# Cross-attention and a mixture of experts on one core: partial sums kept in PSUM by ScalarE copies, and another order of products, silu parts and expert sums

## Chip, core and metric

One core of one Trainium2 chip. The metric is device microseconds of that core for one launch of the kernel. The core's engines are TensorE (PE; its weight loads are PEld), VectorE (DVE), ScalarE (ACT), GpSimd (POOL) and SyncE (SP), which issues the loads and stores. Each runs its own list of instructions in order and waits for the others by semaphores. Matmul results land in PSUM, which has eight banks; all else that engines read lies in SBUF.

## What is computed

x has 16 rows of 112 tokens with 256 features, `ctx` 16 rows of 375. First cross-attention, then a mixture of 8 experts in which every expert is applied to every token:

```
q = layernorm(x) @ Wq + bq;  k = ctx @ Wk + bk;  v = ctx @ Wv + bv
x = x + softmax(q k^T / 16) v
z = layernorm(x)
cw = softmax(z w_router) * softmax(z w_gating / 0.1);  cw = cw / (sum(cw) + 1e-9)
h_e = silu(z w_gate[e]) * (z w_up[e])          # 256 -> 1024, for e = 0..7
x = x + sum_e cw[:, e] * (h_e w_down[e])       # 1024 -> 256
```

## The kernel before

**The head.** `Line` is a small planner: every operation of the attention, of routing and of the first products is declared with an engine, a cost, a priority and what it reads and writes, and `Line.run` writes out an order for each engine from these. `batch(b)` declares the attention of one row: scores, the largest score (`top`, L931), the shift (`low`, L934), the exponential (L938), the transposed probabilities (L944), the mixed context (L957), projection and residual (L972, L979), layer norm and its transposed copy. `port=True` tells the planner that VectorE and GpSimd can't do this beside each other. `top`, `low`, `cs` and `total` are small SBUF tiles.

**The expert steps.** The 1792 tokens are two halves (h) of 896. A step is (expert e, half h, block j of 256 hidden features, m): m = 0 is the gate, m = 1 the up projection; 8 x 2 x 4 x 2 = 128 steps. In a step the product of a 896 x 256 and a 256 x 256 matrix is done with seven products of half-size blocks instead of eight (a scheme of Strassen's kind): `PROD` says which block or sum of blocks of x (`X_...`) and of the weights (`W_...`) go into each. Each product is three matmuls of 448 columns, because every operand is split into a high and a low part (`hi`, `lo`) and the products high-high, low-high and high-low are summed (`PASSES`). The four blocks of the result are

```
(0,0) = P1 + P2            (0,1) = P1 + P6 + P5 + P3   # c12
(1,1) = P1 + P6 + P7 + P5  (1,0) = P1 + P6 + P7 + P4   # c22, c21
```

Before, `step` issues the products in the order 1, 6, 5, 2, 7, 4, 3. ScalarE copies P1 to SBUF (`v1`, L542); VectorE adds up `w16` = P1 + P6 (L547), `u3` = w16 + P7 (L568), `c22` = u3 + C (L570, bank C holds P5), `c21` (L582) and, when P3 has been added in bank C, `c12` (L592). Block (0,0) is summed in bank A by the matmuls. In a gate step ScalarE applies silu to each block (L469); in an up step VectorE multiplies the silu parts by the up blocks (L559, L584, L494), ScalarE casts the result to its high part `hhi` (L488, L495) and VectorE subtracts for the low part `hlo` (L489, L496). What is not done at once is kept in `carry` and issued later by `finish`.

**Down products.** After each up step 14 groups (7 token tiles t, 2 feature halves F) are queued in `downs`; a group is three matmuls of 256 columns (L402). `fill(k)` puts k groups between the products of later steps, seven a step; `KEEP` groups stay in the queue. They sum over the four j in four banks D0 to D3, two token tiles a bank. When an expert's half is complete, `gather` adds it with its weight `cw` to `acc`, on VectorE (L421) or, with `aside`, by ScalarE (L418) and GpSimd (L419).

**Weights.** `plan` sets when a weight is loaded (`raw`), its block sums are formed on GpSimd (`t`, L320 to L323), its high part is cast on ScalarE (`hi`, L335) and its low part subtracted on GpSimd (`lo`, L341); the same for `w_down` (L348, L350). In the first expert one weight is prepared in each step; weights 0 to 2 (`EARLY`) are prepared in the head. `REST` and `offer` slip pieces of the second half's x sums and splits into the first steps.

Of the kernel before, what the change touches and what calls it, by code (L numbers as in the profile page):

```python
# [143 lines left out]
def kernel(  # L144
# [65 lines left out]
    AHEAD = {"w": 16, "d": 16, "hhi": 48, "hlo": 32}  # L210
# [148 lines left out]
    for k in range(NW):  # L359
        e, i = divmod(k, PER)  # L360
        if e == 0:
            if i < EARLY:
                continue
            n = i - 2
            plan(n - 1, "raw", k)
        else:
            n = 2 * PER * (e - 1) + PER + (2, 4, 6, 7, 8, 10, 12, 13)[i]
            plan(n - 2, "raw", k)
        plan(n if e == 0 else n - 1, "t", k)
        plan(n, "hi", k)  # L370
        plan(n + 1, "lo", k)
# [37 lines left out]
    def gather(bank, aside=False):  # L409

        if len(done.get(bank, ())) < min(2, NTT - 2 * bank):
            return
        for h, e, t, pd in done.pop(bank):
            tt = h * NTT + t
            w = cw[:, tt, e : e + 1]
            if aside:
                y = buf("y", [P, D], f"y{h}_{e}_{t}")
                nc.scalar.activation(y, pd, AF.Copy, scale=w)  # L418
                nc.gpsimd.tensor_add(acc[tt], acc[tt], y)  # L419
            else:  # L420
                nc.vector.scalar_tensor_tensor(  # L421
                    acc[tt], pd, w, acc[tt], op0=ALU.mult, op1=ALU.add
                )
        if e == E - 1:
            t0 = (h * NTT + 2 * bank) * P
            a = accs[h, bank]
            nc.sync.dma_start(
                out_f[t0 : t0 + a.shape[1] * P, :].rearrange("(t p) d -> p t d", p=P), a
            )
# [11 lines left out]
    KEEP = 6  # L441
# [25 lines left out]
    def silu(n, blk, src):  # L467
        s = tmp("s", f"{n}s") if blk == (0, 0) else src
# [22 lines left out]
    def put_off(hid, blk, src):  # L491
        s = sg[blk]
        hi, lo = parts(hid, blk)
        carry["hf%d%d" % blk] = lambda: nc.vector.tensor_mul(s, s, src)  # L494
        carry["hhi%d%d" % blk] = lambda: nc.scalar.copy(hi, s)  # L495
        carry["hlo%d%d" % blk] = lambda: nc.vector.tensor_sub(lo, s, f(hi))  # L496

# [11 lines left out]
    def step(n):  # L509
        e, h, j, m = steps[n]  # L510
        up = m == 1
        for what in ("lo", "raw", "rawd", "t"):
            due(n, what)
        hi_now = list(todo.get((n, "hi"), ()))
        todo.pop((n, "hi"), None)
# [5 lines left out]
        if up:  # L521
            hid = [
                (
                    buf("hhi", [P, HT], f"hhi{n}_{F}", FR),
                    buf("hlo", [P, HT], f"hlo{n}_{F}", FR),
                )
                for F in range(2)
            ]
        pb, pc, pe = (psum(t, f"p{t}{n}")[:, :N] for t in "BCE")
        if n > 1:  # L530
            pa = psum("A", f"pA{n}")[:, :N]
        finish("hf10", "hf01")
        if up:
            finish("hlo11")
            gather(1)
        offer()
        if n == 1:
            pa, v1 = e0["pa1"], e0["v11"]
        else:
            prod(n, pa, 1, True, False)  # L540
            v1 = tmp("v1", n)
            nc.scalar.copy(v1, pa)  # L542
        finish("silu01", "hhi10", "hhi01")
        offer()
        prod(n, pb, 6, True, True)
        w16 = tmp("s", f"{n}w")
        nc.vector.tensor_add(w16, v1, pb)  # L547
        if up:
            finish("hlo10")
            newest[0] = n  # L550
        else:
            finish("hlo00", "hlo01")
            gather(2, True)
        hi(0)
        prod(n, pc, 5, True, False)
        fill(1, not up)
        prod(n, pa, 2, False, True)
        if up:
            nc.vector.tensor_mul(sg[(0, 0)], sg[(0, 0)], pa)  # L559
            hi(1)  # L560
            due(n, "d")
        else:
            silu(n, (0, 0), pa)
            gather(3, True)
            hi(1)
# [4 lines left out]
        nc.vector.tensor_add(c22, u3, pc)  # L570
        offer()
        fill(2)
        offer()
        fill(1)
        if up:
            keep_hidden(hid, (0, 0))
        else:
            gather(0)
            silu(n, (1, 1), c22)
        prod(n, pb, 4, True, True)  # L580
        c21 = u3
        nc.vector.tensor_add(c21, u3, pb)  # L582
        if up:
            nc.vector.tensor_mul(sg[(1, 1)], sg[(1, 1)], c22)  # L584
            keep_hidden(hid, (1, 1))
        else:
            silu(n, (1, 0), c21)
        offer()
        fill(2)
        prod(n, pc, 3, False, True)  # L590
        c12 = w16
        nc.vector.tensor_add(c12, w16, pc)  # L592
        fill(1)
        offer()
        if up:
            for blk, src in (((1, 0), c21), ((0, 1), c12)):
                put_off(hid, blk, src)
        else:
            carry["silu01"] = lambda: silu(n, (0, 1), c12)
        if up:  # L600
            T_OF = (range(0, 3), range(4, NTT), range(3, 4))
            order = [(0, t) for t in T_OF[0]]
            order += [(1, t) for t in T_OF[1]]
            order += [(0, t) for t in T_OF[1]] + [(0, 3)]
            order += [(1, t) for t in T_OF[0]] + [(1, 3)]
            if n == len(steps) - 1:
                order.append(order.pop(order.index((0, NTT - 1))))
            seen = set()
            for F, t in order:
                last = j == NJ - 1 and t in seen  # L610
                seen.add(t)

                downs.append((n, h, e * NJ + j, 1 - F, t, hid[F], j == 0, last))
# [34 lines left out]
    top, low, total = (many(n, B) for n in ("top", "low", "total"))  # L648
# [248 lines left out]
    def batch(b):  # L897
# [10 lines left out]

        def turn(k):
# [11 lines left out]
        def score():  # L921
            for k in range(KC):
# [8 lines left out]
           lambda: nc.vector.reduce_max(top[:TQ, col], bank(("sc", b), [TQ, TK]), axis=AX.X, negate=True),  # L931
# [3 lines left out]
               low[:TQ, col], top[:TQ, col], cs[:TQ, col], cs[:TQ, col], op0=ALU.subtract, op1=ALU.add),  # L935
           reads=(("mx", b), ("c", g)), writes=(("nb", b),), port=True)
# [199 lines left out]
    for k in range(EARLY):  # L1136
# [7 lines left out]
        for part in range(2):  # L1144
            op("POOL", (1.02, 1.31)[part], pri, lambda k=k, part=part: load_lo(k, part),
               reads=(("wh", k), ("raw", k), ("t", k)), writes=(("w", k),))
    op("SP", 0.45, 9, lambda: load_rawd(0), writes=("rawd",), waits=("bq", "bk"), kb=256)
# [42 lines left out]
    def silu0():  # L1190
        silu(0, (0, 0), e0["A"])
# [20 lines left out]
    op("PE", 0.61, 31, second, reads=(("w", 1), ("xs", 0, X_A11)), new=(("bank", ("second",), BANKS[4:]),))  # L1212
    op("ACT", 0.54, 31, v1_second, reads=(("second",), "v1"), writes=("v11",), waits=[("aT", B - 1), ("aTl", B - 1)])
# [7 lines left out]
    def later(what, *blocks):  # L1221
# [3 lines left out]
        1: [later(sum_x, X_S1), later(split_hi, X_A22), later(split_hi, X_S1), later(sum_x, X_S2),  # L1225
            later(split_lo, X_A22, X_S1), later(split_hi, X_S2)],
        2: [later(sum_x, X_S3), later(split_lo, X_S2), later(split_hi, X_S3), later(sum_x, X_S4),
            later(split_hi, X_S4)],
        4: [later(split_lo, X_S3), later(split_lo, X_S4)],
# [8 lines left out]
    for n in range(1, len(steps)):  # L1238
        if n in REST:
            waiting.append(parts_of(REST[n]))  # L1240
        step(n)
# [3 lines left out]
    finish("hlo00", "hf10", "hlo11", "hhi10", "hf01", "hhi01", "hlo10", "hlo01")  # L1245
# [41 lines left out]
```

## Time and profile before

| | |
|---|---|
| runs (median; lowest to highest) | 989.07 us; 988.94 to 991.05 |
| profiled execution: time / span | 990.8 us / 989.0 us |
| busy: TensorE / VectorE / ScalarE / GpSimd | 972.8 / 804.3 / 504.7 / 415.7 us |
| matmuls | 6059 |
| granted TensorE clock, mean | 0.998 |

The profile is one execution. A row of the groups names line, engine, operation, output and inputs by the program's names, the shape, the count, busy time and the mean length. The chain that ended last is followed back from the last instruction to whatever released each. A row of the waits is: who waited, for whom, total us, times, longest. A row of a timeline is: start us, length us, engine, line, operation. Successive matmuls overlap: a 448-column matmul is listed with 0.36 us while the next starts 0.20 us later.

### The profile page before, as it was taken

Reading aid. Unit: us, or ns where it says so; the run is one execution under the profiler, and the core shown is the slowest. Engines: PE = TensorE matmul, PEld = TensorE weight load, DVE = VectorE, ACT = ScalarE, POOL = GpSimd, SP = SyncE. Lnnn points to the kernel's source line nnn. Section 1 sums busy time; section 2 is a strip of 40 time slices with the busy share of each in tenths; the row PEclk is TensorE's granted clock in tenths of the full one; section 3 lists DMA queues with packets and bytes.
Section 4 is the critical chain, followed back from the end, with each engine's and each line's share of the span. In section 5 each row is a group of like instructions: output and inputs, shape, how many; then the busy total and the mean of one; then the engine's idle time right before and its main releaser. Section 6 shows DMA issues by size and latency. Waiting matters only on the chain.

```text
span 989.0 us, 16353 instructions
## 1 busy us (share of the span) xinstructions
PE 972.8 (98%) x6059; PEld 907.4 (92%) x6059; DVE 804.3 (81%) x1506; ACT 504.7 (51%) x1037; POOL 415.7 (42%) x524
## 2 busy tenths in 40 slices
PE   9999879999999999999999999999999999999998
PEld 6887769999999999999999999999999999999997
DVE  5778798878888888888887887878888888788786
ACT  5676654455444554555445544456455545455342
POOL 3346483255414561446324550555244632455000
PEclk9999999999999999999999999999999999999999
DMA  9611111001100110011100110011001110010011
GB/s 238 178 48 36 31 43 44 12 22 54 43 2 22 54 33 22 22 33 43 32 12 22 54 44 1 23 54 32 22 22 33 43 32 12 22 44 1 1 38 38
DMA packets 36053, 38.66 MB, mean 39 GB/s; under 512 B 3251, under 2 KB 33974, under 8 KB 35974
## 3 DMA queue, kind: packets, MB, share of 16 engines
q1 hardware_dynamic: 35696, 37.37, 13.1%
q8 instruction: 47, 0.77, 0.3%
q14 instruction: 32, 0.26, 0.1%
q10 hardware_dynamic: 278, 0.27, 0.1%
HBM read 33.95 MB, written 1.84 MB: 36 GB/s over the span
## 4 chain that ended last, share of the span: by engine, by line
PE 94%; DVE 3%; ACT 1%; issue 1%; DMA 0%; POOL 0%; DVEq 0%
PE pd L402 32%; PE pC L436 16%; PE pB L436 15%; PE pA L436 15%; PE pE L436 8%; PE ps_aa L957 2%; PE ps_sc L923 2%; PE ps_qk L869 1%; PE ps_po L972 1%; PE ps_cT L911 1%; PE ps_pp L944 0%; DVE low L934 0%; DMA wn<-in_L_xattn_Wq_dram 0%; PE ps_lg L1048 0%; PE ps_xT L856 0%
## 5 line engine op out<-in xcount | busy, mean ns | idle before, releaser
L402 PE MATMUL pd<-wd,hhi 128*128 128x256 f32 x1792 | 338.8, 280 | 0.0
L402 PEld LDWEIGHTS pd<-wd,hhi 128*128 128x128 f32 x1792 | 308.9, 188 | 14.2
L402 PE MATMUL pd<-wd,hlo 128*128 128x256 f32 x896 | 250.8, 280 | 1.7 <-DVE hlo L489 1.7
L436 PE MATMUL pC<-xs_hi,w 128*128 128x448 f32 x508 | 187.8, 370 | 3.5 <-DVE s_1c L570 0.8
L436 PE MATMUL pB<-xs_hi,w 128*128 128x448 f32 x508 | 186.7, 368 | 0.0
L436 PE MATMUL pA<-xs_hi,w 128*128 128x448 f32 x504 | 183.0, 363 | 0.0
L402 PEld LDWEIGHTS pd<-wd,hlo 128*128 128x128 f32 x896 | 169.2, 189 | 2.0 <-DVE hlo L489 1.9
L419 POOL TENSOR_TENSOR acc<-acc,y 128x256 f32<-128x256 f32 x45 | 35.8, 824 | 247.6 <-ACT y L418 247.6
L341 POOL TENSOR_TENSOR w<-raw,w 128x384 fp32r<-128x384 f32 x64 | 72.8, 1138 | 135.9 <-ACT w L335 135.9
L542 ACT COPY v<-pA 128x448 f32<-128x448 f32 x126 | 67.0, 532 | 89.2 <-PE pA L436 89.2
L436 PEld LDWEIGHTS pC<-xs_hi,w 128*128 128x128 f32 x508 | 95.6, 188 | 14.5 <-DVE s_1c L570 1.2
L436 PEld LDWEIGHTS pB<-xs_hi,w 128*128 128x128 f32 x508 | 96.0, 189 | 5.8 <-DVE s_1u L582 0.2
L436 PEld LDWEIGHTS pA<-xs_hi,w 128*128 128x128 f32 x504 | 94.5, 187 | 4.0 <-ACT v L542 0.3
L436 PE MATMUL pC<-xs_lo,w 128*128 128x448 f32 x254 | 92.7, 365 | 0.0
L436 PE MATMUL pE<-xs_hi,w 128*128 128x448 f32 x254 | 92.5, 364 | 0.0
L436 PE MATMUL pB<-xs_lo,w 128*128 128x448 f32 x254 | 92.1, 363 | 0.0
L436 PE MATMUL pA<-xs_lo,w 128*128 128x448 f32 x252 | 90.9, 361 | 0.0
L341 POOL TENSOR_TENSOR w<-tt,w 128x512 fp32r<-128x512 f32 x64 | 83.1, 1298 | 2.1
L350 POOL TENSOR_TENSOR wd<-rawd,wd 128x512 fp32r<-128x512 f32 x32 | 41.7, 1304 | 72.2 <-ACT wd L348 72.2
L436 PEld LDWEIGHTS pE<-xs_hi,w 128*128 128x128 f32 x254 | 47.7, 188 | 3.2
L436 PEld LDWEIGHTS pC<-xs_lo,w 128*128 128x128 f32 x254 | 47.9, 189 | 1.5
L436 PEld LDWEIGHTS pB<-xs_lo,w 128*128 128x128 f32 x254 | 47.7, 188 | 1.6
(1812 smaller groups left out, 1898.9 us busy)
## 6 DMA issues: line engine op xcount, KB each, us to landing
raw<-in_L_ffn_w_gate_dram SPq DMA_DIRECT2D x32, 256.0 KB
raw<-in_L_ffn_w_up_dram SPq DMA_DIRECT2D x32, 256.0 KB
rawd<-in_L_ffn_w_down_dram SPq DMA_DIRECT2D x32, 256.0 KB
ctx<-in_ctx_dram SPq DMA_DIRECT2D x13, 336.0 KB
out_dram<-acc SPq DMA_DIRECT2D x6, 256.0 KB
wide<-in_x_dram SPq DMA_DIRECT2D x3, 448.0 KB
wide<-in_ctx_dram SPq DMA_DIRECT2D x3, 336.0 KB
ctx<-in_ctx_dram SPq DMA_DIRECT2D x13, 39.0 KB
```

Source lines behind the costliest of these rows:

```text
L341: nc.gpsimd.tensor_sub(wts[k][1][:, d], w, f(wts[k][0][:, d]))
L350: nc.gpsimd.tensor_sub(wds[q][1], rawds[q], f(wds[q][0]))
L402: nc.tensor.matmul(pd, hs[a][:, t * P : (t + 1) * P], wds[q][w][:, fi, :], start=(opening and s == 0), stop=(last and s == 2), skip_group_ ...
L419: nc.gpsimd.tensor_add(acc[tt], acc[tt], y)
L436: nc.tensor.matmul(ps, w_[w][:, wi, :], (xs_hi, xs_lo)[a][h][xi], start=(start and s == 0), stop=(stop and s == 2), skip_group_check=True,)
L542: nc.scalar.copy(v1, pa)
L869: nc.tensor.matmul(bank(("qk", g, m, 0), [P, GT]), m_sb[:, k, m * P : (m + 1) * P], xnT_b[k], start=(k == 0), stop=(k == KC - 1),)
L911: nc.tensor.transpose(bank(("cT", b, k), [P, TK])[:, c * KT : (c + 1) * KT], ct()[:, c, k * P : (k + 1) * P], ident[:KT, :KT],)
L923: nc.tensor.matmul(bank(("sc", b), [TQ, TK]), own(qk_b[k], ("qk", g, k))[:, i * TQ : (i + 1) * TQ], ctT(k), start=(k == 0), stop=(k == KC ...
L957: nc.tensor.matmul(bank(("aa", b), [P, KC, TQ])[:, k, :], ct()[:, c, k * P : (k + 1) * P], pT()[:, c, :], start=(c == 0), stop=(c == NK - 1),)
L972: nc.tensor.matmul(bank(("po", b), [TQ, D]), aT()[:, a, k, :], (wv_hi, wv_lo)[w][:, k, :], start=(k == 0 and s == 0), stop=(k == KC - 1 an ...
```

## The change

- In a step from the third on, ScalarE copies bank A (P1) into bank B, and P6 is added there by its matmuls; ScalarE copies bank B (P1 + P6) into bank E, where P7 and, after `c22` has been read, P4 are added. VectorE no longer adds `u3` and `c21`; it copies bank B to SBUF (`w16`), ScalarE copies P5 to SBUF (`p5`), and VectorE forms `c12` = w16 + C and `c22` = p5 + E. Block (1,0) is read from bank E.
- The order of products is 1, 5, 6, 2, 3, 7, 4; the down groups stand as two after 5, one after 3, four after 7. In a gate step only groups of older pairs are used.
- The second step (n = 1) has its own function, `second_step`, with sums in SBUF as before.
- The low parts of the hidden blocks are subtracted in other places, most of them in the next gate step; `put_off` is gone.
- `gather` is always VectorE's; the calls stand elsewhere. The order of the 14 down groups is another one; `KEEP` is 7.
- In the head `top` lies in the scores' own bank instead of SBUF, `low` reads it there, and `low` is declared without `port`. Weight 3 is loaded and its block sums are formed in the head; in the first expert `raw` and `t` come a step earlier. `REST` starts at step 3.

In the built order of the new program TensorE has as many matmuls as before; VectorE's list has 204 instructions fewer, ScalarE's 204 more, GpSimd's 45 fewer. VectorE's copy `w16` waits for ScalarE's copy of bank B to bank E. In the head GpSimd's sums of weight 3 stand between the low part of weight 1 and the next row statistics.

```diff
-    AHEAD = {"w": 16, "d": 16, "hhi": 48, "hlo": 32}
+    AHEAD = {"w": 32, "d": 16, "hhi": 48, "hlo": 32}
...
             n = i - 2
-            plan(n - 1, "raw", k)
+            if i > EARLY:
+                plan(n - 2, "raw", k)
...
-        plan(n if e == 0 else n - 1, "t", k)
+        if k > EARLY:
+            plan(n - 1, "t", k)
...
-    KEEP = 6
+    KEEP = 7
...
+    def leave(hid, blk):
+        hi, lo = parts(hid, blk)
+        s = sg[blk]
+        carry["hhi%d%d" % blk] = lambda: nc.scalar.copy(hi, s)
+        carry["hlo%d%d" % blk] = lambda: nc.vector.tensor_sub(lo, s, f(hi))
+
+    def hide(blk, src):
+        nc.vector.tensor_mul(sg[blk], sg[blk], src)
...
     def step(n):
         e, h, j, m = steps[n]
         up = m == 1
+        hi, hid = begin(n)
+        pb, pc, pe = (psum(t, f"p{t}{n}")[:, :N] for t in "BCE")
+        pa = psum("A", f"pA{n}")[:, :N]
+        if up:
+            gather(2)
+            gather(3)
+        offer()
+        prod(n, pa, 1, True, False)
+        nc.scalar.copy(pb, pa)
+        offer()
+        prod(n, pc, 5, True, False)
+        p5 = tmp("v1", f"{n}p5")
+        nc.scalar.copy(p5, pc)
+        if up:
+            newest[0] = n
+        else:
+            if n > 2:
+                finish("hhi11", "hlo00", "hlo01")
+            gather(0)
+        fill(2, not up)
+        prod(n, pb, 6, False, True)
+        nc.scalar.copy(pe, pb)
+        w16 = tmp("v1", f"{n}w")
+        nc.vector.tensor_copy(w16, pb)
+        if n == 2:
+            hi(0)
+        finish("hhi01", "hhi11", "hhi10")
+        if n > 2:
+            hi(0)
+        offer()
+        prod(n, pa, 2, False, True)
+        if up:
+            hide((0, 0), pa)
+            hi(1)
+            due(n, "d")
+        else:
+            silu(n, (0, 0), pa, False)
+            hi(1)
+        prod(n, pc, 3, False, True)
+        c12 = tmp("s", f"{n}c12")
+        nc.vector.tensor_add(c12, w16, pc)
+        offer()
+        fill(1, not up)
+        prod(n, pe, 7, False, False)
+        if up:
+            keep_hidden(hid, (0, 0))
+        else:
+            silu(n, (0, 1), c12)
+        c22 = tmp("s", f"{n}c22")
+        nc.vector.tensor_add(c22, p5, pe)
+        offer()
+        if up:
+            hide((0, 1), c12)
+            keep_hidden(hid, (0, 1))
+        else:
+            finish("hlo00", "hlo01", "hlo11", "hlo10")
+        fill(4, not up)
+        if not up:
+            gather(1)
+        prod(n, pe, 4, False, True)
+        if up:
+            hide((1, 1), c22)
+            leave(hid, (1, 1))
+            hide((1, 0), pe)
+            leave(hid, (1, 0))
+            queue_downs(n, hid)
+        else:
+            silu(n, (1, 1), c22)
+            silu(n, (1, 0), pe, False)
+        offer()
...
+        order = [(0, t) for t in range(3)] + [(1, t) for t in range(NTT)] + [(0, t) for t in range(3, NTT)]
...
+        top = lambda: bank(("sc", b), [TQ, 512])[:, TK : TK + 1]
...
-               low[:TQ, col], top[:TQ, col], cs[:TQ, col], cs[:TQ, col], op0=ALU.subtract, op1=ALU.add),
-           reads=(("mx", b), ("c", g)), writes=(("nb", b),), port=True)
+               low[:TQ, col], top(), cs[:TQ, col], cs[:TQ, col], op0=ALU.subtract, op1=ALU.add),
+           reads=(("sc", b), ("mx", b), ("c", g)), writes=(("nb", b),))
...
+    op("SP", 0.45, 11, lambda: load_raw(EARLY), new=(("raw", ("raw", EARLY)),), kb=256)
+    op("POOL", 1.9, 29.5, lambda: load_t(EARLY), reads=(("raw", EARLY),), new=(("tt", ("t", EARLY)),))
...
-        1: [later(sum_x, X_S1), later(split_hi, X_A22), later(split_hi, X_S1), later(sum_x, X_S2),
-            later(split_lo, X_A22, X_S1), later(split_hi, X_S2)],
-        2: [later(sum_x, X_S3), later(split_lo, X_S2), later(split_hi, X_S3), later(sum_x, X_S4),
-            later(split_hi, X_S4)],
-        4: [later(split_lo, X_S3), later(split_lo, X_S4)],
+        3: [later(sum_x, X_S1, X_S2), later(split_hi, X_A22, X_S1), later(split_lo, X_A22), later(sum_x, X_S3),
+            later(split_hi, X_S2), later(sum_x, X_S4)],
+        4: [later(split_lo, X_S1), later(split_hi, X_S3), later(split_lo, X_S2), later(split_hi, X_S4),
+            later(split_lo, X_S3), later(split_lo, X_S4)],
...
-        step(n)
+        step(n) if n > 1 else second_step()
```

## Prediction

> **What bounds the kernel now.** I read the page first. TensorE is busy for 98% of the span and is 94% of the chain that ended last, so the change can win only where TensorE stands still, and it can lose wherever a new wait opens.
>
> ```profile
> PE 972.8 (98%) x6059; PEld 907.4 (92%) x6059; DVE 804.3 (81%) x1506; ACT 504.7 (51%) x1037; POOL 415.7 (42%) x524
> ...
> PE 94%; DVE 3%; ACT 1%; issue 1%; DMA 0%; POOL 0%; DVEq 0%
> ```
>
> Next the chain in order of time (start, length, what). A run of nine down matmuls occurs once per step, so the distance between two of them is a step.
>
> ```profile
> 206.91 1.06 PE pd L402 x9
> 213.62 1.06 PE pd L402 x9
> 220.33 1.06 PE pd L402 x9
> 227.24 1.06 PE pd L402 x9
> 233.95 1.06 PE pd L402 x9
> ```
>
> A step takes 6.71 us, and now and then 6.9. Successive matmuls of a product start 0.20 us apart and down matmuls 0.118 us (1.06/9), so a step's bare work is 21 x 0.20 + 21 x 0.118 = 6.68 us: it has no room. From 153 us to the end 15 steps are long, by 0.175 us on average: 2.6 us. In each of the two per expert, the multiply of L584 took 1.61 us instead of 0.62 while GpSimd ran, the add of L592 behind it came late, and the next product 5 waited for bank C.
>
> Then TensorE's waits (total, times, longest). They lie almost all between 93 and 149 us, where attention ends and the expert steps begin.
>
> ```profile
> PE ps_sc L923 <- DVE s L628: 2.3, 2, 1.4
> PE pd L402 <- DVE hlo L489: 1.7, 1, 1.7
> ...
> PE ps_pp L944 <- ACT s L938: 0.9, 1, 0.9
> PE pC L436 <- DVE s_1c L570: 0.8, 1, 0.8
> PE ps_first_C L436 <- DVE s_0c L1177: 0.8, 1, 0.8
> PE pC L436 <- DVE s_3c L570: 0.8, 1, 0.8
> PE pC L436 <- DVE s_3w L592: 0.7, 1, 0.7
> ```
>
> Last the timeline of VectorE around 100 us, then GpSimd's in the same stretch.
>
> ```profile
> 100.24 3.66 DVE L934 SCALAR_TENSOR_TENSOR low<-top,cs 112x1 f32<-112x1 f32 x1
> 104.40 0.22 DVE L934 SCALAR_TENSOR_TENSOR low<-top,cs 112x1 f32<-112x1 f32 x1
> ```
>
> ```profile
> 99.48 1.00 POOL L341 TENSOR_TENSOR w<-raw,w 128x384 fp32r<-128x384 f32 x1
> 100.44 1.27 POOL L341 TENSOR_TENSOR w<-tt,w 128x512 fp32r<-128x512 f32 x1
> 101.67 2.22 POOL L286 TENSOR_TENSOR xs_lo<-wide,xs_hi 128x448 fp32r<-128x448 f32 x2
> ```
>
> An operation on one column, 0.22 us when free, is held until GpSimd's row of work is over. The exponentials and TensorE stand behind it.
>
> **Part 1: `top` in PSUM.** `low` then has one tensor input in SBUF. The Trainium skill, "SBUF — State Buffer", section "Who interferes with whom", says that a VectorE instruction with at most one SBUF input does not contend with GpSimd, and that one with two is blocked for a GpSimd instruction. The row agrees on who is held, not on how long: by the rule at most one instruction, 1.27 us; measured 3.66 - 0.22 = 3.4 us, over four. I use the row. The holds at 94.6 us (2.15) and 100.2 us made TensorE wait 1.37 us (the longer of the L923 waits) and 0.90 us (L944): **-2.3 us**. By the rule the second hold alone would shrink to about 1 us and this wait would be nearly nothing before, so -1.4. What is late next is the last batch's layer norm, which still needs GpSimd. The planner reorders the head with it and puts four GpSimd operations (about 1.9 us, four starts 0.41 to 0.53 apart) for weight 3 there; before, GpSimd stood idle for 2.27 us at 96.7, which covers them. Without that cover: +1. Bounds -4 to +1.
>
> **Part 2: the steady step.** Matmuls are the same in number (2688 of products, 2688 down). Per step VectorE does one copy and two adds instead of five adds; over 126 steps 252 operations of 0.62 us fewer, 156 us, and 45 weighted sums at 0.474 more, 21 us: some 670 us busy. ScalarE gets two more copies of 0.53 a step (134 us) and loses 45 evictions of 0.48 (22): some 617 us. Neither fills up; only the chain inside a step matters. I lay a step out from its first matmul at 0. In the trace of before an engine starts 0.46 us after the start of the last matmul that it waits for (pA 500.21, ScalarE's copy 500.67).
>
> TensorE: product 1 at 0, product 5 at 0.60, two down groups (0.354 each) at 1.20, product 6 at 1.91, product 2 at 2.51, product 3 at 3.11, one group at 3.71, product 7 at 4.06, four groups at 4.66, product 4 at 6.08. The weight load that carries a wait stands 0.12 us ahead of its matmul after down groups.
>
> Copy A to B: 0.40 + 0.46 = 0.86, to 1.39; needed at 1.79: **0.40 us of slack**. Behind it on ScalarE the copy of product 5 (1.46 to 1.99), which product 3 needs at 2.9. Copy B to E: 2.31 + 0.46 = 2.77, to 3.30; needed at 3.94. Weight casts, hidden copies and silus queue behind these, and in a gate step with casts ScalarE's list is 3 x 0.53 + 2 x 0.57 + 4 x 0.57 + 1.13 = 6.1 of 6.7 us; the last silu waits for product 4 (6.94) and ends at 7.5, when the next copy A to B is due at 7.57.
>
> VectorE: `w16` copies B as well. Here the skill speaks against the change: "PSUM — Partial Sum Buffer", section on bank collisions, says that two engines must not read one bank together. No row of before shows such a pair; the built program indeed makes this copy wait for ScalarE. Without the rule it would start at 2.77, by it at 3.35. I take 3.35. In an up step: to 3.89 (starts are 0.54 apart), multiply by pA to 4.43, `c12` to 4.97, `c22` 4.97 to 5.60. Product 4's weights may load at 5.96: **0.3 us of slack** (0.9 by the earlier start). Product 4 is the step's last work, so a late `c22` delays everything queued on TensorE.
>
> ScalarE copying PSUM to PSUM is in no row. Nearest: L542, PSUM to SBUF, 0.53; between 0.35 and 0.93 nothing changes, so I take 0.53 and no stall. The two-input SBUF operations that GpSimd can hold (now the second and third multiply and four `hlo` subtractions) stand after `c22` or before `w16`, with about 2 us between; the 1 us delay of L584 fits. Product 5 no longer reads a bank that a late add still holds (`c12` is done 2 us before). So the 15 long steps go: **-2.6 us** (0 to -2.6; a further -1 to -2 is open because down groups come in three lots instead of four).
>
> The tightest spot: the up step after a half's last gate step. All expert sums are now on VectorE; seven of 0.43 us, five of them just ahead of this step's `w16`. From 5.46 in the gate step: two subtractions that GpSimd holds to about 8.0, then five sums to 10.2, which is 3.5 in the up step; `c22` is ready at 5.7. It still fits, by 0.25.
>
> **Part 3: steps 1 to 4.** Before, from product 7 of step 1 (122.54) to step 5 (149.47) it took 26.9 us, with 15 down groups done. Now, counting from the same T: product 3 of step 1 waits for `c22` as before and ends at T+2.4. The three multiplies in SBUF then run beside GpSimd (in before such ones took 0.9 to 1.7) to about T+7.0; `w16`, `c12`, `c22` follow to 8.7, so product 4 of step 2, which has no down groups (old ones do not exist yet), ends at T+9.4. Step 3 runs seven groups at once, which covers ScalarE's backlog, then waits about 1.4 us for `c22`: T+17.8. Step 4 is full: T+24.5, with 14 groups done, one fewer: 24.9. **-2.0 us** (-4 to +1). Moving the second half's sums and splits (REST) to steps 3 and 4 puts 4 us of GpSimd work into step 4, needed only at step 8: nothing.
>
> **Part 4: the end.** The new order of sums leaves banks 1 to 3 for the last four groups; VectorE's five sums end about 1.4 us after TensorE instead of 1.07 (984.81 to 985.88): **+0.3**. Keeping seven groups instead of six covers the last splits.
>
> Sum: -2.3 - 2.6 - 2.0 + 0.3 = -6.6. The profiled execution took 990.8 us with a span of 989.0; the median of the runs is 989.07. Against the profiled one the sum gives 984.2; the median is 1.7 us lower, and I forecast against it: **982.5 us**.
>
> **Rivals.** (A) Slower: the copy A to B does not fit. It decides from 0.93 us a copy. At 1.05 us product 6 waits 0.12 us in each of 126 steps, +15 us, 997.6. For it: no row shows ScalarE writing PSUM. Against: 0.53 is far off. 7%. (B) The sums ahead of `w16` push `c22` past 5.96 in 15 up steps, by 0.45 each: +6.8, 989.3: no change. The 3.66 us hold speaks for it, the operations that alternate with GpSimd at 0.7 to 1.1 us against. 9%. (C) Head and first steps give nothing (GpSimd's queue and step 2 without down groups eat it); only the long steps go: about 987. 9%. (D) Better: fewer changes between matmul shapes save 0.02 us a step and the slow matmuls at 119 us (0.37 apart) vanish: 978.5. 7%.
>
> **Numbers.** The likeliest case, 68%, spans 979 to 986.5. The range 977 to 990 leaves out A and the tails. 0.2% (2 us) is about what can be told from no change. Faster: likeliest, D, half of C: 0.80; same: B, half of C: 0.13; slower: 0.07.
>
> **What would show it.** Right: `low` at 0.2 us throughout; steps of 6.7 us without long ones; TensorE's waits of steps 1 to 4 near 4 us together; copies A to B of about 0.5 us. Wrong: a wait of TensorE for pB or pE in every step (A), for c22 twice an expert (B), or waits between 93 and 125 us as long as before (C).

## The result and the profile after

The changed kernel takes 972.82 us (median of four runs, 971.75 to 975.84); the kernel before, run beside it, 989.87 (with one run more than in the table above). The ratio is 0.9832, with a 95% interval of 0.9806 to 0.9858: faster by 17 us, where 6.6 was forecast, and below the forecast range of 977 to 990. Run again in a later comparison it took 974.92 us (973.37 to 976.38), ratio 0.9846 [0.9831, 0.9860]. The profiled execution of after took 975.84 us with a span of 974.0, against 989.0 before: 15.0 us to account for.

The page of after, busy time and the share of engines in the chain that ended last:

```profile
PE 961.8 (99%) x6059; PEld 904.0 (93%) x6059; DVE 721.3 (74%) x1302; ACT 610.8 (63%) x1241; POOL 393.1 (40%) x479
...
PE 98%; DVE 1%; DMA 0%; issue 0%; DVEq 0%
```

TensorE has the same 6059 matmuls but is busy for 11 us less. Busy time alone doesn't say why: a matmul of 448 columns is listed 0.16 us longer than its distance to the next, so a delay that short counts as busy. The chain shows the distances themselves. This is the chain of after, one full step and the start of the next (a step has one run of twelve down matmuls; the chain of before stands in the prediction):

```profile
206.58 1.39 PE pd L404 x12
207.97 0.60 PE pE L432 x3
208.57 0.60 PE pA L432 x3
209.17 0.60 PE pC L432 x3
209.78 0.71 PE pd L404 x6
210.48 0.61 PE pB L432 x3
211.09 0.60 PE pA L432 x3
211.69 0.60 PE pC L432 x3
...
212.65 0.60 PE pE L432 x3
213.25 1.39 PE pd L404 x12
```

A step takes 6.67 us (213.25 - 206.58), and there are no long ones: over 119 steps the mean is 6.673. Before, a plain step took 6.713 and the mean with the long ones was 6.734. TensorE's waits (total, times, longest) now:

```profile
PE pE L432 <- DVE s_3c L617: 2.6, 1, 2.6
PE pE L432 <- DVE s_2c L617: 1.7, 1, 1.7
PE idle L726 <- DVE nhalf L223: 1.2, 1, 1.2
...
PE pC L432 <- DVE s_1c L547: 0.8, 1, 0.8
PE pC L432 <- DVE s_1w L554: 0.3, 1, 0.3
PE pB L432 <- ACT pB L576: 0.2, 1, 0.2
```

All waits on VectorE and ScalarE that remain, but the one at the start, are in steps 1 to 4; nothing waits in the steady steps. The head's waits for scores and probabilities are gone, and `low` is short all through, here as a group in before and then in after (count | busy, mean ns):

```profile
L934 DVE SCALAR_TENSOR_TENSOR low<-top,cs 112x1 f32<-112x1 f32 x16 | 10.3, 656 | 0.2
```

```profile
L970 DVE SCALAR_TENSOR_TENSOR low<-ps_sc,cs 112x1 f32<-112x1 f32 x16 | 3.4, 215 | 0.4
```

I cut both spans at two marks: T, the start of the last matmul of product 7 in step 1, and the start of step 5.

| stretch, us | before | after | difference | forecast |
|---|---|---|---|---|
| start to T | 122.54 | 115.53 | -7.0 | -2.3 |
| T to step 5 (one down group more, 0.35, before) | 26.93 | 26.13 | -0.45 without the group | -2.0 |
| step 5 to the end (the group is done here) | 839.5 | 832.4 | -7.5 without the group | -2.6 + 0.3 |

The last row is 123 steps: (6.734 - 6.713) x 123 = 2.6 for the long steps and (6.713 - 6.673) x 123 = 4.9 for the pitch of all of them. The end itself changed by nothing: VectorE's last sums end 1.07 us after TensorE in both.

### The profile page after: what moved, and what is told of

The parts are those of the page before. It is cut to its first block, busy times and chain, and to the rows that moved or that the text cites. A ratio compares the mean times of both kernels' runs of the same rounds, so it can differ in the third digit from the quotient of the medians.

```text
span 974.0 us, 16070 instructions
## 1 busy us (share of the span) xinstructions
PE 961.8 (99%) x6059; PEld 904.0 (93%) x6059; DVE 721.3 (74%) x1302; ACT 610.8 (63%) x1241; POOL 393.1 (40%) x479
## 4 chain that ended last, share of the span: by engine, by line
PE 98%; DVE 1%; DMA 0%; issue 0%; DVEq 0%
PE pd L404 32%; PE pE L432 16%; PE pC L432 16%; PE pA L432 15%; PE pB L432 8%; PE ps_aa L993 2%; PE ps_sc L959 2%; PE ps_qk L903 1%; PE ps_po L1008 1%; PE ps_cT L947 1%; PE ps_pp L980 1%; PE ps_lg L1084 1%; DMA wn<-in_L_xattn_Wq_dram 0%; PE ps_xT L890 0%; PE ps_xx L1055 0%; DVE s_0c L523 0%
## 5 line engine op out<-in xcount | busy, mean ns | idle before, releaser
L404 PE MATMUL pd<-wd,hhi 128*128 128x256 f32 x1792 | 330.4, 279 | 0.0
L404 PEld LDWEIGHTS pd<-wd,hhi 128*128 128x128 f32 x1792 | 299.8, 188 | 10.1
L432 PE MATMUL pE<-xs_hi,w 128*128 128x448 f32 x506 | 184.4, 364 | 4.3 <-DVE s_3c L617 2.6
L589 ACT COPY pE<-pB 128x448 f32<-128x448 f32 x126 | 65.2, 517 | 69.3 <-PE pB L432 69.1
L432 PEld LDWEIGHTS pE<-xs_hi,w 128*128 128x128 f32 x506 | 95.0, 188 | 8.3 <-DVE s_3c L617 2.9
L432 PE MATMUL pB<-xs_hi,w 128*128 128x448 f32 x256 | 93.7, 366 | 0.2 <-ACT pB L576 0.2
L576 ACT COPY pB<-pA 128x448 f32<-128x448 f32 x126 | 65.2, 517 | 43.6 <-PE pA L432 40.2
L432 PE MATMUL pE<-xs_lo,w 128*128 128x448 f32 x253 | 91.5, 362 | 0.0
L432 PEld LDWEIGHTS pB<-xs_hi,w 128*128 128x128 f32 x256 | 48.7, 190 | 2.7 <-ACT pB L576 0.6
L432 PEld LDWEIGHTS pA<-xs_lo,w 128*128 128x128 f32 x252 | 47.2, 187 | 3.4
```

What stands on the lines that cost most here:

```text
L404: nc.tensor.matmul(pd, hs[a][:, t * P : (t + 1) * P], wds[q][w][:, fi, :], start=(opening and s == 0), stop=(last and s == 2), skip_group_ ...
L432: nc.tensor.matmul(ps, w_[w][:, wi, :], (xs_hi, xs_lo)[a][h][xi], start=(start and s == 0), stop=(stop and s == 2), skip_group_check=True,)
L576: nc.scalar.copy(pb, pa)
L589: nc.scalar.copy(pe, pb)
```

## The experiments

My theory after the result: three terms of unequal kind, the head (-7), the long steps (-2.6) and a shorter pitch of the matmuls (-5); the rivals are the sizes of the forecast, and that the sums in PSUM are one cause of all. Times are medians, ratios are to the kernel before on the same chip.

### Only `top` in PSUM

```diff
-    top, low, total = (many(n, B) for n in ("top", "low", "total"))
+    low, total = (many(n, B) for n in ("low", "total"))
+        top = lambda: bank(("sc", b), [TQ, 512])[:, TK : TK + 1]
...
-               low[:TQ, col], top[:TQ, col], cs[:TQ, col], cs[:TQ, col], op0=ALU.subtract, op1=ALU.add),
-           reads=(("mx", b), ("c", g)), writes=(("nb", b),), port=True)
+               low[:TQ, col], top(), cs[:TQ, col], cs[:TQ, col], op0=ALU.subtract, op1=ALU.add),
+           reads=(("sc", b), ("mx", b), ("c", g)), writes=(("nb", b),))
```

> The kernel before, with only top moved to the scores' bank (and low declared without port), so that low can't be held by GpSimd; the planner orders the head anew from that. Between the profiles of before and after, product 7 of step 1 came 7.0 us earlier, where 2.3 was forecast. Theory: the held operation was nearly all of it, since the waits behind it (0.78, 0.40 and 0.43 us), the 0.9 us at 78.5 and the slow matmuls at 119 us hang on it too. Then product 7 of step 1 starts near 116.5 us instead of 122.5, low takes 0.22 us throughout, and the time is about 984 (-6). Rival: only the two waits of 1.37 and 0.90 hang on it and the rest came with the earlier weight 3 and the other order of the first steps: 987.5 (-2.3).

Measured: 983.88 us, ratio 0.9940 [0.9919, 0.9962]. `low` took 0.22 us throughout, T came at 113.53 (9.0 earlier), the wait for `c22` in step 1 grew from 0.8 to 1.9 us, and step 5 began at 141.55 instead of 149.47. The head alone is worth about 6 us (0.6%); the 2.3 of the forecast is out. This kernel's tiles also lie 64 bytes lower; with them put back (under "The old order at other addresses") the gain is 4.6 us.

### The changed kernel with `top` back in SBUF

The same edit the other way round.

> The changed kernel with top back in SBUF and port=True. Theory: the head loses 5 to 7 us again, 978 to 980 against 972.8, with low held by GpSimd for microseconds at least once. Rival (the earlier weight 3 and the other planner order made the head short): at most 2 us more, 973 to 975.

Measured: 989.47 us, ratio 0.9999: the whole gain was gone, more than any of the theories gave. Two things had changed. `low` took up to 4.07 us again, and T stood at 122.22. But the steady step was 6.720 us too, with the same instructions there: products of 0.604 to 0.613 us instead of 0.600 to 0.610, and 1.411 instead of 1.396 us for the twelve down matmuls. I had not foreseen it. What differs there is where the tiles lie: `top` takes 64 bytes of every SBUF partition, so all tiles from the weights on lie 64 bytes higher. The line of the diff that I had passed over, `AHEAD` with 32 instead of 16 columns of unused fp32 ahead of the weights, makes up for these 64 bytes: in the built programs the weight tiles of before and after start at the same address, 137600, and here at 137664.

### The multiply of L584 put off

In a long step of before VectorE's multiply was held and the add of bank C stood behind it:

```profile
222.58 1.61 DVE L584 TENSOR_TENSOR s_14c<-s_14c,s_15c 128x448 f32<-128x448 f32 x1
224.12 0.61 DVE L592 TENSOR_TENSOR s_15w<-s_15w,pC 128x448 f32<-128x448 f32 x1
```

```diff
-            nc.vector.tensor_mul(sg[(1, 1)], sg[(1, 1)], c22)
-            keep_hidden(hid, (1, 1))
+            put_off(hid, (1, 1), c22)    # finished in the next step, as the other blocks
```

> The kernel before, with the multiply of block (1,1) (L584) put off behind the step's last add, into the next step, as the other two already are. Theory: the 15 long steps came from this multiply, which GpSimd holds for 1 us ahead of the add of bank C; without it ahead all steps are 6.71 us and the time is 2.6 us less, 986.5 to 987. Rival: the add is late for other reasons (VectorE is full at 81%), the long steps stay or go elsewhere, 989 to 991.

Measured: 988.37 us, ratio 0.9977 [0.9970, 0.9984], so -1.5 us where 2.6 was expected. All 118 measured steps were 6.71 or 6.72 us, none long, and from step 5 to the end it took 836.9 us, 2.6 less than before: the cause of the long steps is right, and so is their worth. Ahead of them one wait grew, for which before has 1.7 us (from TensorE's waits); two for bank C in steps 1 and 3 (0.6 and 0.7) went, and step 5 began 0.4 us later:

```profile
PE pd L402 <- DVE hlo L489: 3.2, 1, 3.2
```

### Both parts together in the old order

`top` in PSUM, the spacer at 32 and L584 put off, in the kernel before; no sums by ScalarE, the old order and lots.

> The kernel before with top in PSUM, the spacer at 32 (so that the weights keep their addresses) and the multiply of L584 put off to the next step, the two parts that gained alone. No sums in PSUM by ScalarE, the old order of products and the old four lots. Theory that the parts add up and that the rest of the gain lies in the pitch of the steps, which only the new order has: steps of 6.713 us without long ones, so -5 for the head and -2.6 for the long steps, less the wait for hlo that opens at the start when L584 is put off (up to 2 us): 980.5 to 983.5 us. Rival (the sums in PSUM save nothing by themselves; the two parts together also give the rest): 972 to 976.

Measured: 981.23 us, ratio 0.9917 [0.9902, 0.9933]; steps of 6.713 us. Step 5 began at 141.93 and the rest took 837.6 us, 5.2 more than in after (832.4). So the two parts give 9.3 us of the 15.6 that after gained in this comparison (990.55 to 981.23 and to 974.92), and the rest lies in the steps (0.040 x 123 = 4.9). The new order that it comes with is several edits at once: ScalarE's sums in PSUM, the order of the products, the lots, the order of the 14 groups. Only the lots were tried by themselves, so how much the sums in PSUM give is not shown.

### The number of lots

The changed kernel with its seven down groups in four lots, in two lots, and in three lots of other sizes:

```diff
-        fill(4, not up)                  # lots 2, 1, 4: after products 5, 3, 7
+        fill(3, not up)                  # four lots: 2, 1, 1, 3 (one more after product 2)
...
-        fill(2, not up)
+        fill(3, not up)                  # two lots: 3 after 5, none after 3, 4 after 7
...
+        fill(2, not up)                  # three lots: 2 after 5, 2 after 3, 3 after 7
```

> The changed kernel with its seven down groups of a step in four lots instead of three (2 after product 5, 1 after 2, 1 after 3, 3 after 7). The step fell from 6.714 to 6.675 us, 5 us over the run. Theory: changing between 448- and 256-column matmuls costs about 0.01 to 0.015 us a time on TensorE, and the change has one lot fewer; then the step here is 6.69, the time 2 us above the changed kernel, about 975. Rival: the shorter step comes from the order of products and fewer VectorE reads of PSUM: the step stays at 6.675 and the time at 973.

Measured: 979.82 us, ratio 0.9901; a step of 6.720 us. That looked like 0.047 us for one more lot, and I took it for the price of a change of matmul shape.

> The changed kernel with the seven down groups of a step in two lots (three after product 5, four after product 7) instead of three (2, 1, 4). Theory that each change between the matmul shapes costs about 0.04 us a step (what four lots instead of three cost): a step of 6.63 us, 123 steps, 5 us less: 967 to 969 us. Rival 1 (the cost of four lots was not the count but where the lots stand): no change, 972 to 974. Rival 2: product 7 follows product 3 at once, so the copy of bank B to bank E has 0.35 us less time; by my layout it ends at 3.65 us of the step and is needed at 3.94, so no new wait; if there is one, a wait of TensorE for pE in each step and 975 us or more.

Measured: 978.91 us, ratio 0.9884 [0.9870, 0.9898], and the plain step was 6.687 us: fewer lots and slower. The price per lot falls. (Every eighth step or so was longer by another 0.05, 6.695 in the mean.)

> The changed kernel with its three lots of down groups at the same places but 2, 2 and 3 groups instead of 2, 1 and 4. Count theory (each lot costs about 0.045 us): 6.673 us a step as in the changed kernel, 972 to 974 us. Rival, which the two-lot kernel speaks for (6.687 a step, not 6.63): the pitch hangs on how matmuls of the two shapes and the addresses fall together, and every kernel so far has a step of 6.72 us less a multiple of 0.0067: any value from 6.66 to 6.72, most likely not 6.673; 973 to 979 us.

Measured: 979.67 us, ratio 0.9896; a step of 6.693 us with the same number of lots. So it isn't the count alone.

### Addresses alone

Only numbers of `AHEAD` differ; no instruction, wait or order does. The spacer at 32 is the changed kernel.

```diff
-    AHEAD = {"w": 32, "d": 16, "hhi": 48, "hlo": 32}
+    AHEAD = {"w": 16, "d": 16, "hhi": 48, "hlo": 32}   # all from the weights on 64 bytes lower
...
+    AHEAD = {"w": 48, "d": 16, "hhi": 48, "hlo": 32}   # 64 bytes higher
+    AHEAD = {"w": 64, "d": 16, "hhi": 48, "hlo": 32}   # 128 bytes higher
+    AHEAD = {"w": 48, "d": 16, "hhi": 32, "hlo": 32}   # only the weights 64 bytes higher
+    AHEAD = {"w": 32, "d": 32, "hhi": 48, "hlo": 32}   # the down weights, and what lies behind them, 64 bytes higher
```

> The changed kernel with one edit: the unused spacer ahead of the weight tiles (AHEAD, w) back from 32 to 16 columns. No instruction, wait or order changes; every tile from the weights on lies 64 bytes lower in each SBUF partition, where removing the SBUF tile top puts it without the wider spacer. Address theory (the products are slower when these tiles start at an odd multiple of 64 bytes, as in the two kernels that moved top): products of 0.61 us instead of 0.60, a step of about 6.72 instead of 6.673 us, 978 to 980 us in all. Rival (addresses are nothing; what slowed the steps of the kernel with top back in SBUF is something that top or low do): 972 to 974 us, the step 6.67.

> The changed kernel with the spacer ahead of the weights at 48 columns instead of 32: all tiles from the weights on lie 64 bytes higher, as in the kernel with top back in SBUF, whose step took 6.720 us. Address theory: a step of 6.720 us, 978 to 980 us, with the head of the changed kernel. Rival (the 6.720 came from top and low, and the spacer there only happened to undo it): 6.673, 973 to 975.

> The changed kernel with the spacer at 64 columns: the same tiles 128 bytes higher. 64 bytes lower gave a step of 6.687 us, 64 higher 6.720. If the pitch repeats every 128 bytes those two would be equal, and they are not, so I expect another value still, 6.68 to 6.72 us, 974 to 980 us. A period of 128 bytes would give 6.673.

> The changed kernel with only the weight tiles 64 bytes higher (spacer w 48, spacer hhi 32, so that all tiles behind the weights stay). The weight tiles are what the products load; the down groups load hhi and hlo and stream the down weights. If the products' pitch comes from their own weights' address: products at 0.608 to 0.613 us as with top in SBUF, lots as in the changed kernel, a step of 6.72 or a little more. Rival (the address of other tiles does it): 0.600 and 6.673.

> The changed kernel with only the down weights' tiles 64 bytes higher (spacer d 32 instead of 16; only rawd lies behind them). If the lots' pitch comes from the address of the operand that they stream: lots other than 0.709, 0.351 and 1.395 us, products as in the changed kernel. Rival (only loaded operands matter, hidden parts and weights): the step stays 6.673 us.

| tiles moved | steady step, us | time, us |
|---|---|---|
| none (the changed kernel) | 6.673 | 972.82 and 974.92 |
| all, 64 bytes lower | 6.687 | 976.86 |
| all, 64 higher | 6.720 | 979.37 |
| all, 128 higher | 6.673 | 974.89 |
| only the weights, 64 higher | 6.740 | 983.00 |
| only the down weights, 64 higher * | 6.720 | 981.25 |

\* In the built program `rawd`, `raw` and `tt`, which lie behind them, move too; in these steps TensorE reads none of them.

The steps compare better than the times, which hold the head and the first steps as well. The first expectation had the direction right and the size too high (0.013 us a step, not 0.047); the third was wrong, since at 128 bytes the step has the same length again. That is no period of 128 bytes, though: 64 lower and 64 higher lie 128 bytes apart and differ by 0.033 us a step. A step of the kernel with only the weights moved, from its chain:

```profile
200.86 0.60 PE pE L432 x3
201.46 0.61 PE pA L432 x3
202.07 0.60 PE pC L432 x3
202.67 0.71 PE pd L404 x6
203.38 0.62 PE pB L432 x3
204.00 0.62 PE pA L432 x3
204.62 0.62 PE pC L432 x3
205.24 0.36 PE pd L404 x3
205.59 0.61 PE pE L432 x3
206.21 1.39 PE pd L404 x12
```

Beside the step of after above: the three products behind the lot of six are 0.62 instead of 0.60 or 0.61; the lots are the same to 0.01. With only the down weights moved it was the other way: the twelve took 1.43 us instead of 1.395, and no product changed by more than 0.01 (the same lot as in the last line above):

```profile
206.28 1.43 PE pd L404 x12
```

### `top` in SBUF at the right addresses

The changed kernel with `top` back in SBUF and the spacer back at 16, so that the weights start at 137600 again.

> The changed kernel with top back in SBUF (and low held by GpSimd again), and the spacer ahead of the weights back to 16 columns, so that the weight tiles keep the changed kernel's addresses. It ran at 989.5 us with the spacer at 32. Address theory: the step comes back to 6.67 us, low and the head stay as slow as before (first product's end near 122 us), so 979.5 to 983 us, and the difference of this run to the changed kernel, 7 to 9 us, is what top alone is worth. Rival (addresses are nothing): 989 us again, the step 6.72.

Measured: 985.0 us, ratio 0.9946. The step is 6.673 us again and the stretch from step 5 to the end 832.4, exactly as in after. The 16.6 us of the first try are thus two things. The address is worth 5.8 us in the steps (838.15 to 832.36 from step 5 to the end); the medians differ by less, 4.5 us, since in this profile step 5 began 1.4 us later than in the first try. And the spans of this kernel and after, 983.3 and 974.0, differ by 9.3, all of it ahead of step 5 (150.96 against 141.66). Of these 9.3 I estimate 4.5 for matmuls at a lower granted clock, which after's profile doesn't have: 0.50 from 120.5 to 126.0 us and 0.66 from 142 to 147 (5.5 x 0.50 + 5 x 0.34 = 4.5). My 979.5 to 983 did not have them.

### The old order at other addresses

> The kernel before with only top in PSUM (983.9 us), and the spacer ahead of the weights widened to 32 columns, so that the weight tiles keep the addresses of the kernel before. Address theory: its products, 0.607 to 0.623 us with the tiles 64 bytes lower, come back to 0.599 to 0.617, a step of 6.733 us becomes what it was before (6.738 to 6.73), so little: 982.5 to 984, unless the 0.01 us a product that the kernel before shows less of is worth more; with 123 steps of 0.02 to 0.05 us less, 978 to 981. Rival (addresses are nothing): 983.9 again and the same product times.

Measured: 984.96 us (982.5 to 984 expected; 989.52 for before beside it), 6.736 us a step in the mean, the long ones included; at 64 bytes lower it was 6.738. The product times came back as the address theory says (product 1 from 0.613 to 0.600), but the lots grew by nearly as much (the lot of nine from 1.040 to 1.058), and there was hardly a gain: in the old order these 64 bytes move time from one to the other.

> The kernel before with top in PSUM and the put-off multiply (981.2 us, steps of 6.713 us), the tiles from the weights on 64 bytes higher. If the pitch gain of the changed kernel needs its order of products and lots, no address brings the old order below about 6.70 us a step: 980 to 983 us. Rival (the old order only had an unlucky address): 6.67 to 6.69 us, 976 to 979 us.

> The same with the tiles 128 bytes higher. In the changed kernel 128 bytes gave the same step again (6.673 us), so here 6.713 us and 980.5 to 982.5 us. Rival (the equality there was chance): another multiple of 0.0067 us below 6.72, 976 to 982 us.

Measured: 983.73 us (980 to 983 expected) with steps of 6.733, and 982.14 us with steps of 6.707. Together with 6.713 (spacer 32) and 6.72 (64 bytes lower, the plain step with only `top` changed) the old order lies at 6.707 to 6.733, the new one at 6.673 to 6.720 over the same four shifts. The best of the old order is slower than the new one by 0.033 us a step. At 128 bytes higher I had expected 6.713 again and got 6.707, another multiple, as the rival said. Only these four shifts of all tiles were tried.

### The piece of x sums ahead of `c22`

In step 3 of after a piece of the second half's x sums stood between `c12` and `c22` on VectorE and was held to 1.43 us. I put it behind `c22`. VectorE's timeline in after, then in this kernel:

```diff
         nc.vector.tensor_add(c12, w16, pc)
-        offer()
+        if n != 3:
+            offer()
...
-        offer()                          # behind c22
+        offer(2 if n == 3 else 1)
```

```profile
131.57 0.61 DVE L608 TENSOR_TENSOR s_3c<-v_3w,pC 128x448 f32<-128x448 f32 x1
132.10 1.43 DVE L275 TENSOR_TENSOR sx<-wide 128x224 f32<-128x224 f32 x1
133.45 0.61 DVE L617 TENSOR_TENSOR s_3c<-v_3p,pE 128x448 f32<-128x448 f32 x1
133.99 2.52 DVE L523 TENSOR_TENSOR s_2c<-s_2c,s_3c 128x448 f32<-128x448 f32 x2
```

```profile
130.02 0.61 DVE L618 TENSOR_TENSOR s_3c<-v_3p,pE 128x448 f32<-128x448 f32 x1
130.55 0.91 DVE L275 TENSOR_TENSOR sx<-wide 128x224 f32<-128x224 f32 x1
131.38 3.05 DVE L523 TENSOR_TENSOR s_2c<-s_2c,s_3c 128x448 f32<-128x448 f32 x2
```

> The changed kernel with one piece of the second half's x sums (L275) taken from between c12 and c22 of step 3 and put behind c22. It took 1.43 us there (GpSimd held it) and c22, for which TensorE waits 2.6 us, stood behind it. Theory that this term made the first steps gain so little: the wait for s_3c falls from 2.6 to 1.2 us, and the whole is 1 to 1.4 us faster than the changed kernel of the same batch, 971 to 972 us. Rival (the multiplies of step 3, pushed back by the same piece, bring the time back at the next down groups): the wait moves to pd or to pE of step 4, no difference.

Measured: 973.76 us, ratio 0.9842 [0.9828, 0.9856], beside 974.92 for after in the same comparison; their intervals overlap, so the 1 to 1.4 us expected are neither shown nor excluded by the times. The wait for `s_3c` fell from 2.5 to 1.2 us as expected. From T to step 5 it still took 26.16 us (113.43 to 139.59) against 26.13 in after: step 4 now waits 0.5 us for its `c22` and 0.4 for bank B. The profile is the rival's: the wait moved on by a step.

### The changed kernel once more

> The changed kernel once more, not edited, for a tighter time beside the kernels of this batch: 971.5 to 974 us, every step from the sixth on 6.673 us.

Measured: 974.92 us, a little above the 971.5 to 974 expected; 6.673 us a step, 832.4 us from step 5 to the end. Its T came 2.1 us sooner than in the first profile, but T to step 5 took 28.8 us instead of 26.1. The stretch that starts behind the same 2.5 us wait for `s_3c` shows why; each row is stretch, length, busy time of PE, PEld, DVE, ACT and POOL, granted clock, DMA share and GB/s. This run, then the first profile of after over the same work:

```profile
132.00:138.30 6.30, 6.28 (x20) 5.75 (x21) 4.99 (x6) 2.49 (x6) 6.14 (x9) 0.51 0.31 83
```

```profile
134.10:140.40 6.30, 6.28 (x38) 6.01 (x39) 6.20 (x9) 4.92 (x12) 6.14 (x9) 1.00 0.28 83
```

In 6.30 us there are 20 matmuls instead of 38, at a granted clock of 0.51 instead of 1.00. The Trainium skill, "TensorE: Matmul & The Clock Gate", section "Part 1: The HAM clock gate", says that an idle window, about 3.4 us, halves the array's clock until a busy window has passed, and that the windows run free of the program, so that the cost differs from run to run. The difference between runs agrees: same program, same wait, 2.7 us apart. The length doesn't: TensorE's longest wait in these two profiles was 2.6 us, behind shorter ones, so what was counted as idle these runs don't show. Among the eleven profiles of kernels with this head and these first steps (the lots, addresses and x sums changed) five have such a stretch at a lower clock behind step 3, and T to step 5 is 27.3 to 28.8 us there; in the other six it is 26.1 to 26.2.

Another part of the spread comes at the very start. The first `low` begins at 19.1 to 23.1 us in these profiles, at 21.1 in this one and 23.1 in the first of after, which makes nearly all of the 2.1 us of T.

## Why the prediction was wrong, point by point

**What bounds it: right.** TensorE's own work set the time, and all gains were on it. The ScalarE copies fit: L576 and L589 took 0.517 us a piece where I took 0.53, and no steady step waits for them. Rivals A and B did not come.

**Part 1, the head (-2.3; measured -7.0 to T): the mechanism right, the size wrong.** The failed step is "made TensorE wait 1.37 us ... and 0.90 us: -2.3". I summed what TensorE showed as waits at the two longest holds, but the last row's chain was the path, and it lost the holds in full. All `low` in before, in after and with only `top` changed (shortest/median/longest in ns, first and last start):

```profile
L934 DVE SCALAR_TENSOR_TENSOR low<-top,cs x16: 198/220/3662, 22.2 to 104.4; 112x1 f32<-112x1 f32 x16
```

```profile
L970 DVE SCALAR_TENSOR_TENSOR low<-ps_sc,cs x16: 198/219/219, 23.1 to 98.5; 112x1 f32<-112x1 f32 x16
```

```profile
L936 DVE SCALAR_TENSOR_TENSOR low<-ps_sc,cs x16: 198/218/220, 21.1 to 96.4; 112x1 f32<-112x1 f32 x16
```

The three profiles don't start alike, so count from the first `low`. The last one then starts after 82.2 us in before and 75.3 to 75.4 in the others: 6.8 to 6.9 us, which is what all the holds add up to (10.3 - 3.4 = 6.9 in the groups above; the two long ones are 5.4 of it). Order has a part as well: in the changed kernel with `top` back in SBUF the holds are 7.4 and the last `low` comes 9.0 us later. T comes after 100.3 us in before and 92.4 in both others: 7.9 us. So `top` alone gives the head's whole gain up to T, and the earlier weight 3 adds nothing that shows. The 1 us between 6.9 and 7.9, I estimate, is what before loses in a stretch at half clock just ahead of T; before, then after over the same times (same columns):

```profile
118.90:121.50 2.60, 2.60 (x9) 2.34 (x9) 1.60 (x4) 1.53 (x4) 1.07 (x3) 0.50 0.03 6
```

```profile
118.90:121.50 2.60, 2.25 (x10) 1.78 (x11) 2.60 (x3) 2.10 (x6) 2.52 (x3) 1.00 0.22 55
```

In before the matmuls are 0.37 us apart there instead of 0.20, seven times: 1.2 us. I had it only in rival D, at 7%. Whether it belongs to the holds is open: with `top` back in SBUF T came at 122.22 with matmuls 0.20 us apart there. The bound of -4 was too tight for the same reason as the -2.3. And where I weighed the rule of the skill against the row, the row was the better guide to the hold, but I took the wrong number from it: the wait seen beside it.

**Part 2, long steps (-2.6): right**, with 2.6 measured. The layout's estimate for VectorE, 670 us busy, was 51 too low (in after's trace most of its subtractions for `hlo` took 0.9 to 1.6 us instead of 0.62), but nothing waited for it. **The pitch: the second failed step, wrong in size and in cause.** The step's bare work of "6.68 us: it has no room" was taken as given, and the sum has nothing for it; "a further -1 to -2 is open because down groups come in three lots instead of four" stood outside the sum. Measured -4.9. Two lots gave 6.687 us, three 6.673 or 6.693, four 6.720 and, in the old order, 6.707 to 6.733. Every plain step measured here is 6.72 us plus or minus a small multiple of 0.0067 (6.673 is seven less, 6.713 one less, 6.740 three more). What sets the multiple, beyond that order, lots and addresses each move it, these runs don't show.

**Part 3 (-2.0; measured -0.45): the term that was off is step 3's wait**, 1.4 us in the forecast, 2.6 measured, because I had no x sum in front of `c22`. But the run without it shows that the term was not worth its 1.2 us either: removing one delay shows the next. The held multiplies (two of them took 2.5 and 3.1 us in VectorE's rows above, where free ones take 0.62 each) are the likely bound; no run takes them out. Behind the same short head the old first steps took 28.0 to 28.6 us in five profiles, but each has a stretch at a lower clock behind T, so how much better the new ones are stays open.

**Part 4 (+0.3): measured 0.**

**What I left out:** the `AHEAD` line. I quoted it in the change and gave it no step. Without it (spacer at 16) the kernel takes 976.86 us; had the shift gone the other way, 979.37.

## What to carry to other kernels

When an operation on the critical chain is held by another engine, count the whole of every hold, and follow the chain to where the delay comes out; the waits next to it are only part. When a TensorE-bound kernel has no waits left, measure the pitch of its matmuls: an edit that adds or drops an SBUF tile can move it by 0.05 us a step (6 us here), so hold the addresses fixed when you compare, and try a few spacers. A wait of TensorE can cost more than its length, if the clock drops behind it (2.7 us more here), and it may do so in one run and not in the next. Count times in a head from a common event: these profiles start up to 4 us apart.

## What was not expected of the hardware

The pitch of matmuls depends on where their SBUF operands lie, in steps of 64 bytes: 6.673, 6.687, 6.720 and 6.740 us for one and the same list of instructions. The Trainium skill, "TensorE: Matmul & The Clock Gate", section "Step-by-step: what each phase is for", says that TensorE reads the streamed and the loaded operand through two independent ports and that loading doesn't take bandwidth from the running matmul. From that I would not have expected an address to matter; the sentence itself has nothing on addresses, so these runs don't contradict it. Moving only the loaded weights cost 0.067 us a step, moving only the streamed down weights 0.047. Which mechanism it is stays open. Steps are also very even: in each of three kernels (four lots; `top` in SBUF again; only the weights moved) all 118 steps had the same length to 0.01 us.
